# Passage into the second half: small weights ahead of the features, the features in four pieces, a layer's parameters four pieces ahead of their use

## The chip, the cores and the metric

The kernel runs on one core of one Trainium2 chip. A core has a matrix engine (PE, with its weight loads shown as PEld), three engines for elementwise work (DVE, ACT, POOL) and a sync engine, SP, whose queue issues nearly all transfers of this kernel. Each engine executes its own instructions in the order in which the program emitted them; they wait for each other through semaphores. Transfers are carried by 16 DMA engines that all queues share.

The metric is the time of one execution in device microseconds. Before the change it is 5200.37 us, the median of 3 runs (5200.36, 5200.37 and 5221.51).

## The reference

The input x has shape (4, 96, 64, 64). Four layers follow each other:

- Layer 0: two state-space (Mamba) blocks over the 4096 positions, then a 1x1 fusion. The fusion has a global part: the mean of x over the positions goes through `gp_w`, a ReLU and the second half of `fus_w`, and is added per image and channel. A batch norm over all images follows, with a residual:

```python
gp = relu(x.mean((2, 3)) @ gp_w.T + gp_b)
out = einsum('oc,bchw->bohw', fus_w, concatenate([mamba_out, broadcast(gp)], axis=1)) + fus_b
out = (out - mu) * rsqrt(var + EPS) * bn_g + bn_b + residual
```

- Layer 1: a group norm, a 3x3 mean pool (p), and a masked quadratic form over channels, added to its input. For each position and output channel o it sums `weight[o,c,d] * mask[o,c,d] * p[c] * p[d]`.
- Layers 2 and 3: tokens of 96 channels. An attention stand-in (layer norm, a linear map to 192 with batch norm and ReLU, an FFT over the tokens, a diagonal complex map with ReLU, the inverse FFT, a linear map back with batch norm), then a feed-forward part whose operands, weights and biases are rounded to 8-bit floats. Each layer i has its own parameters: `w1`, `w2`, the two batch norms `bn1` and `bn2` (gamma, beta, mean, variance), and the feed-forward weights `fw1`, `fw2` and biases `fb1`, `fb2`.

## The kernel before, in words

`tile_hybrid_kernel` has two halves. `_mamba` computes layer 0 up to the fused features and writes them to a DRAM tensor `fd[b]`, one per image b. `_back` does the rest. Their on-chip buffers come from pools that are closed and opened between the halves, and the first instructions of `_back` that touch a buffer start only when `_mamba` has ended.

**The passage.** `_back` begins with `begin()` (L695) and the first part of `norms(0, ...)` (L772). `begin()` emits, on SP, in this order: image 0's x in two halves (`xb`, L699), the features of image 0 as one transfer (`f`, L701), three 96x96 weights `gp_w`, `fus_g` and `grp` (L702 to L704, through the helper `_load` at L43, so the trace shows them at L45), then 32 loads of the quadratic form's weights and masks (L717), in eight groups of four. Then it emits the chain that makes the batch norm's scale `scl` and shift `shf`, mostly tiny DVE operations (L722 to L754) with two PE matmuls `p_g` (needs `gp_w`, L727) and `p_c` (needs `fus_g`, L731). Last, it emits on POOL, for each of the eight groups, two products of a weight and a mask and a sum (L758 to L760, called `wk`), with two clearings of the padded image `gpad` (L766) after the second group.

`norms(0)` then emits, for eight chunks of 512 columns, f = f * scl + x (DVE, L794) and the statistics of the result (L796), the group norm's scale and shift (L802 to L819, with `grp` in two matmuls), and for each of eight strips y a clearing of border rows on POOL (L838 for the first strip, L840 for the last), a copy into the padded image (ACT, L842), four DVE additions (L845 to L854) and two stores of the pooled strip to DRAM (L856). As soon as the first strip is pooled, `fill` (L863) can load shifted copies of it, the `cp` tiles (L873, L874), into 16 buffers.

**The products of image 0.** Layer 1 is computed as 37 products for each chunk of 512 positions. `product(n)` (L891) makes z for product n+3 on DVE (L887; L884 on ACT for one in 37), loads further `cp` tiles whose buffers are free, and emits the PE matmul of product n (L902), which the trace shows as two PE instructions. The z tiles have five buffers. An image has 8 chunks, so 296 products.

**The order around the change** is written out by hand, not planned: `together` (L1358) takes lanes of pieces and merges them by their relative position. For image 0 there are two lanes: the 296 products, and a side lane with the rest of `norms(0)` (36 pieces), `params(0)` (18), `params(1)` (18), `norms(1)` (61) and an empty stretch of weight 8. That makes 141 weights, so a piece of the side lane comes after every 296/141 = 2.10 products. `through(gen, n)` (L1370) cuts a generator at its `yield`s into n pieces, and the last piece runs whatever is left.

**A layer's parameters.** `params(i)` (L915) prepares one layer. Its pieces, counted by its `yield`s:

- piece 1: loads of `bn1` (L923), `w1` and `w2` (L924 and L925, shown at L45); piece 2 is empty;
- piece 3: 1/sqrt(var + eps) of bn1 times gamma, `s1` (`_rsqrt`, L611, then L929);
- piece 4: w1 times s1 (L932), a PE matmul that centres it (`p_c`, L934), its copy back on ACT (L935);
- piece 5: w1's bias row (L937, L938), load of `bn2` (L940); piece 6 is empty;
- piece 7: the same for bn2 (`s2`); piece 8: w2 times s2 and small vectors (L947 to L957);
- from piece 9: for fw1, fw2, fb1 and fb2 in turn, a load (L964), an empty piece, and two pieces later the rounding (two DVE casts, L968 and L970). The 18 pieces end during this: the last one loads fb2 and rounds it at once.

The loads go into temporary tiles with the tag `zz` (`hold`, L919), of which there are four buffers. `bn1` is loaded with one row per partition, 97 rows of 3072 bytes; `w1` with 97 rows of 768 bytes.

After image 0, the products of image b run beside the token layers of image b-1 (`layers`, L1333), and image 3's token layers run alone at the end.

Of the kernel before, what the change touches and what calls it, by code (L numbers as in the profile page):

```python
# [9 lines left out]
F32 = mybir.dt.float32  # L10
# [17 lines left out]
TC = 512  # L28
NCH = L // TC
H = 192  # L30
# [627 lines left out]
def _back(ctx, tc, io, w, fd, fstats, xsums, p2, out):  # L658
# [28 lines left out]
    def slot(name):  # L687
        return slots.tile([128, NJ * C], F32, name=name, tag="slot")
# [5 lines left out]

    def begin():  # L695

        xb = [slot(f"xb{h}")[0:C, 0 : L // 2] for h in range(2)]
        for h in range(2):
            nc.sync.dma_start(xb[h], io["x"][0][:, h * (L // 2) : (h + 1) * (L // 2)])  # L699
        f = feats[0] = feat.tile([C, L], F32, name="f_0", tag="f")  # L700
        nc.sync.dma_start(f, fd[0])  # L701
        c["gp_w"] = _load(nc, wp, io["gp_wT"], [C, C], "gp_w")  # L702
        c["fus_g"] = _load(nc, wp, io["fus_wT"][C : 2 * C, :], [C, C], "fus_g")
        c["grp"] = _load(nc, wp, io["k_group"], [C, C], "grp")  # L704


        free = [("cp", 0)] * NCP + [("zz", h) for _ in range(4) for h in range(2)] + [("n2", 0)] * 3 + [("z", 0)] * 5
        lds, zz = [], None
        for k0 in range(0, NE, KG):
            kn = min(KG, NE - k0)  # L710
            ld = []
            for m in ("bw1", "bm1", "bw2", "bm2"):
                tag, h = free.pop(0)
                if tag != "zz" or h == 0:
                    zz = tl(f"{m}_{k0}", [128, 2 if tag == "zz" else 1, TC], tag=tag)
                t = zz[:, h, 0 : kn * C].rearrange("p (k c) -> p k c", k=kn)
                nc.sync.dma_start(t, io[m][:, k0 : k0 + kn, :])  # L717
                ld.append(t)
            lds.append(ld)

        xsum = small("xsum")
        nc.vector.tensor_reduce(xsum, xsums, AX.X, ALU.add)  # L722
        fmv = wp.tile([C, B, 2], F32, name="fmv", tag="fmv")
        for b in range(B):
            nc.vector.bn_aggr(fmv[:, b, :], fstats[:, b])
        p_g = bank("s", [C, B], "p_g")
        nc.tensor.matmul(p_g, c["gp_w"], xsum, start=True, stop=True)  # L727
        gp = small("gp")
        nc.scalar.activation(gp, p_g, AF.Relu, bias=vec[:, _V_GPB : _V_GPB + 1], scale=1.0 / L)
# [12 lines left out]
        nc.vector.tensor_tensor(dv, dv, dv, ALU.mult)  # L742
        nc.vector.tensor_tensor(dv, dv, fmv[:, :, 1], ALU.add)
        var = small("var", 1)
        nc.vector.tensor_reduce(var, dv, AX.X, ALU.add)
        nc.vector.tensor_scalar(var, var, 1.0 / B, None, ALU.mult)
        rstd = _rsqrt(nc, work, var, [C, 1], "bn")
        c["scl"] = small("scl", 1)
        nc.vector.tensor_tensor(c["scl"], rstd, vec[:, _V_BNG : _V_BNG + 1], ALU.mult)
        c["shf"] = small("shf")  # L750
        nc.vector.tensor_scalar(c["shf"], cb, mu, c["scl"], ALU.subtract, ALU.mult)
        nc.vector.tensor_scalar(c["shf"], c["shf"], vec[:, _V_BNB : _V_BNB + 1], None, ALU.add)
        c["bias"] = small("bias")
        nc.vector.tensor_scalar(c["bias"], c["shf"], vec[:, _V_L1B : _V_L1B + 1], None, ALU.add)  # L754

        for n, ld in enumerate(lds):
            t = wp.tile([128, KG, C], F32, name=f"wk{n}", tag=f"wk{n}")[:, 0 : ld[0].shape[1]]
            nc.gpsimd.tensor_tensor(t, ld[0], ld[1], ALU.mult)  # L758
            nc.gpsimd.tensor_tensor(ld[2], ld[2], ld[3], ALU.mult)
            nc.gpsimd.tensor_tensor(t, t, ld[2], ALU.add)  # L760
            wk.append(t)
            if n == 1:
                c["gpad"] = []
                for i in range(2):
                    g = wp.tile([C, NY + 2, PW], F32, name=f"gpad{i}", tag=f"gpad{i}")
                    nc.gpsimd.memset(g, 0.0)  # L766
                    c["gpad"].append(g)
        return xb
# [146 lines left out]
    def params(i):  # L915

        d = {}

        def hold(name):  # L919
            return tl(f"{name}_{i}", [128, 2 * TC], tag="zz")  # L920

        bn1 = hold("bn1")[0 : C + 1, 0 : 4 * H].rearrange("p (a h) -> p a h", a=4)
        nc.sync.dma_start(bn1, io["bn1"][i])  # L923
        d["w1"] = _load(nc, wp, io["w1T"][i], [C + 1, H], f"w1_{i}")  # L924
        d["w2"] = _load(nc, wp, io["w2T"][i].rearrange("(h p) c -> p h c", h=2), [C, 2, C], f"w2_{i}")  # L925
        yield
        yield
        s1 = _rsqrt(nc, _Cut(hold("s1")), bn1[:, 3, :], [C + 1, H], f"s1_{i}")
        nc.vector.tensor_tensor(s1, s1, bn1[:, 0, :], ALU.mult)  # L929
        yield  # L930

        nc.vector.tensor_tensor(d["w1"][:C], d["w1"][:C], s1[:C], ALU.mult)  # L932
        p_c = bank("s", [C, H], f"p_c{i}")
        nc.tensor.matmul(p_c, tabs["ctr"], d["w1"][:C], start=True, stop=True)  # L934
        nc.scalar.copy(d["w1"][:C], p_c)  # L935
        yield
        nc.vector.tensor_tensor(s1, s1, bn1[:, 2, :], ALU.mult)  # L937
        nc.vector.tensor_tensor(d["w1"][C:], bn1[C:, 1, :], s1[C:], ALU.subtract)  # L938
        bn2 = hold("bn2")[0:C, 0 : 4 * C].rearrange("p (a h) -> p a h", a=4)
        nc.sync.dma_start(bn2, io["bn2"][i])  # L940
        yield
        yield
        s2 = _rsqrt(nc, _Cut(hold("s2")), bn2[:, 3, :], [C, C], f"s2_{i}")
        nc.vector.tensor_tensor(s2, s2, bn2[:, 0, :], ALU.mult)
        yield
        for h in range(2):
            nc.vector.tensor_tensor(d["w2"][:, h], d["w2"][:, h], s2, ALU.mult)  # L947
        d["sh2"] = wp.tile([1, C], F32, name=f"sh2_{i}", tag=f"sh2_{i}")
        nc.vector.tensor_tensor(d["sh2"], bn2[0:1, 2, :], s2[0:1], ALU.mult)
        nc.vector.tensor_tensor(d["sh2"], bn2[0:1, 1, :], d["sh2"], ALU.subtract)  # L950
        at = _V_ATT + i * 8
        for k, n in enumerate(("rd", "id", "rb", "ib")):
            d[n] = [vec[:, at + 2 * k + h : at + 2 * k + h + 1] for h in range(2)]
        for n, k, f in (("nid", 2, -1.0), ("rb2", 4, 2.0)):
            t = wp.tile([C, 2], F32, name=f"{n}_{i}", tag=f"{n}_{i}")
            nc.vector.tensor_scalar(t, vec[:, at + k : at + k + 2], f, None, ALU.mult)
            d[n] = [t[:, h : h + 1] for h in range(2)]  # L957
        yield

        def quantised(name, src, shape, dtype):  # L960
            n = math.prod(shape[1:])
            view = (lambda t: t) if len(shape) == 2 else (lambda t: t.rearrange("p (k c) -> p k c", k=shape[1]))
            t = view(hold(name + "f")[0 : shape[0], 0:n])
            nc.sync.dma_start(t, src)  # L964
            yield
            yield
            q = view(tl(f"hq_{name}_{i}", [128, NHC * TC], F8)[0 : shape[0], 0:n])
            nc.vector.tensor_copy(q, t, saturate=False)  # L968
            r = wp.tile(shape, dtype, name=f"{name}_{i}", tag=f"{name}_{i}")
            nc.vector.tensor_copy(r, q)  # L970
            d[name] = r
            yield

        yield from quantised("fw1", io["fw1T"][i], [C, HID], BF16)
        yield from quantised("fw2", io["fw2T"][i].rearrange("(h p) c -> p h c", h=NHC), [128, NHC, C], BF16)
        yield from quantised("fb1", io["fb1"][i], [128, NHC], F32)
        yield from quantised("fb2", io["fb2"][i], [128, 4 * C], F16)
        prm.append(d)

    def tables():  # L980
# [401 lines left out]
    with tc.manual_schedule():  # L1382
# [4 lines left out]
        for b in range(B):  # L1387
            lanes = [[(1.0, lambda n=n: product(n)) for n in range(b * NCH * NE, (b + 1) * NCH * NE)]]
            side = []
            if b == 0:  # L1390
                tables()
                side += through(opening, 36) + through(params(0), 18) + through(params(1), 18)
            else:
                lanes.append(idle(5.0) + layers(b - 1, False))
            if b + 1 < B:
# [165 lines left out]
```

## Time and profile before

The profiled execution took 5205.16 us; its span, from the first to the last instruction, is 5203.4 us. All positions below are in us from the start of that span.

| what | value |
|---|---|
| median of the runs | 5200.37 us |
| profiled execution, its span | 5205.16 us, 5203.4 us |
| busy share of the span: PE, DVE, ACT, POOL | 78%, 83%, 52%, 55% |
| passage, from the last store of `_mamba` to image 0's first product | 3052.3 to 3117.3 |
| products of image 0 | 3117 to 3418 |
| in that stretch: PE busy, DVE busy | 271.17 of 301 us, 257.65 of 301 us |
| the same, ACT and POOL busy | 22.22 us, 0.45 us |

A row of the timeline gives the start, the duration, the engine, the line, the operation, its output and inputs, and in brackets the idle time of the engine just before it with what ended the wait. SPq is the issuing of a transfer on SP, not the transfer. The chain of waits is followed back from the last instruction: at each step to what released it.

### The profile page before, as it was taken

Reading aid. Unit: us, or ns where it says so; the run is one execution under the profiler, and the core shown is the slowest. Engines: PE = TensorE matmul, PEld = TensorE weight load, DVE = VectorE, ACT = ScalarE, POOL = GpSimd, SP = SyncE. Lnnn points to the kernel's source line nnn. Section 1 sums busy time; section 2 is a strip of 40 time slices with the busy share of each in tenths; the row PEclk is TensorE's granted clock in tenths of the full one; section 3 lists DMA queues with packets and bytes.
Section 4 is the critical chain, followed back from the end, with each engine's and each line's share of the span. In section 5 each row is a group of like instructions: output and inputs, shape, how many; then the busy total and the mean of one; then the engine's idle time right before and its main releaser. Section 6 shows DMA issues by size and latency. Waiting matters only on the chain. (4 is left out here: it accounts for less than half of the span.)

```text
span 5203.4 us, 52872 instructions
## 1 busy us (share of the span) xinstructions
PE 4082.1 (78%) x15440; PEld 1752.6 (34%) x15440; DVE 4317.2 (83%) x5639; ACT 2680.5 (52%) x5149; POOL 2849.5 (55%) x2105
## 2 busy tenths in 40 slices
PE   4667877777777778777776728998898898989776
PEld 2222222222222222222222103345455454545565
DVE  2879999999999999999999778979787978787655
ACT  3555665656566665656565410025453444434566
POOL 2768888888888888888888650003130312212122
PEclk7777777777787777777786659999999999999877
DMA  4768888888988888898888754653324333232110
GB/s 111 170 157 207 194 202 206 195 206 194 214 193 201 200 204 206 194 213 191 203 198 207 171 144 142 194 152 94 105 79 145 94 92 111 87 94 81 47 33 21
DMA packets 314048, 800.20 MB, mean 154 GB/s; under 512 B 52247, under 2 KB 58106, under 8 KB 312702
## 3 DMA queue, kind: packets, MB, share of 16 engines
q1 hardware_dynamic: 310174, 790.53, 60.6%
q10 hardware_dynamic: 3584, 6.29, 0.4%
q8 instruction: 123, 2.02, 0.2%
q14 instruction: 167, 1.37, 0.1%
HBM read 703.83 MB, written 67.63 MB: 148 GB/s over the span
## 5 line engine op out<-in xcount | busy, mean ns | idle before, releaser
L475 POOL TENSOR_TENSOR hs<-hs,bc 128x1024 f32<-128x1024 f32 x767 | 1666.4, 2180 | 391.6 <-DVE hs L469 387.1
L469 DVE TENSOR_TENSOR_SCAN hs<-a,hst,pq 128x512 f32<-128x512 f32 x1280 | 1571.4, 1261 | 9.8 <-ACT a L452 9.8
L902 PE MATMUL py<-z,wk 128*96 128x512 f32 x2304 | 1114.8, 613 | 22.1 <-issue 14.3
L457 DVE TENSOR_TENSOR pq<-pq,bc 128x1024 f32<-128x1024 f32 x640 | 775.2, 1211 | 233.3 <-PE pq L447 233.2
L887 DVE TENSOR_TENSOR z<-cp,cp 128x512 f32<-128x512 f32 x1152 | 790.2, 711 | 185.9 <-PE py L902 173.4
L452 ACT ACTIVATE a<-a,aneg 128x512 f32<-128x512 f32 x1280 | 843.9, 711 | 38.4 <-DMA a<-ddl 33.1
L488 PE MATMUL py<-hs,red 128*32 128x512 f32 x3072 | 663.0, 855 | 29.8 <-POOL hs L475 29.5
L902 PEld LDWEIGHTS py<-z,wk 128*96 128x96 f32 x2304 | 366.9, 169 | 446.4 <-issue 315.1
L447 PE MATMUL pq<-uy,sel 64*128 64x512 f32 x768 | 258.2, 637 | 201.4 <-DVE hs L469 200.4
L1152 POOL MEMSET zz<- 96x2 f32 x16 | 1.6, 98 | 745.6 <-ACT zz L1161 651.8
L264 PE MATMUL mm_i<-hn,wk 97*128 97x512 f32 x512 | 322.8, 763 | 106.1 <-ACT xcv L275 80.9
L1253 POOL TENSOR_TENSOR o<-o,fb 128x384 f16<-128x384 f16 x64 | 70.0, 1094 | 546.6 <-ACT o L1258 493.3
L452 ACT ACTIVATE pq<-a,aneg 128x512 f32<-128x512 f32 x256 | 177.0, 692 | 334.0 <-DVE hs L469 322.8
L469 DVE TENSOR_TENSOR_SCAN hs<-pq,hst,db 128x512 f32<-128x512 f32 x256 | 323.7, 1264 | 3.5 <-POOL dx L303 1.5
L275 ACT ACTIVATE xcv<-mm_i,pvec 128x512 f32<-128x512 f32 x96 | 66.0, 687 | 493.4 <-DVE y L496 244.0
L457 POOL TENSOR_TENSOR db<-db,bc 128x1024 f32<-128x1024 f32 x128 | 301.6, 2356 | 14.3 <-DMA db<-ddu 14.3
L447 PE MATMUL pq<-ux,sel 64*128 64x512 f32 x512 | 175.6, 631 | 124.8 <-DMA ux<-ul 65.0
L447 PEld LDWEIGHTS pq<-uy,sel 64*128 64x128 f32 x768 | 98.9, 236 | 477.5 <-DVE hs L469 350.8
L264 PEld LDWEIGHTS mm_i<-hn,wk 97*128 97x128 f32 x512 | 106.8, 232 | 293.0 <-issue 161.0
L1184 PE MATMUL px<-bd,a 128*96 128x128 f32 x1024 | 147.6, 292 | 70.9 <-DVE a L1117 61.6
L1153 POOL TENSOR_TENSOR zz<-zz 96x256 f32<-96x256 f32 x128 | 122.6, 958 | 135.8 <-ACT zz L1160 83.6
L447 PEld LDWEIGHTS pq<-ux,sel 64*128 64x128 f32 x512 | 68.0, 229 | 326.4 <-DVE hs L469 178.8
(286 smaller groups left out, 6532.7 us busy)
## 6 DMA issues: line engine op xcount, KB each, us to landing
a<-ddl SPq DMA_DIRECT2D x768, 512.0 KB, 6.3
cp<-p SPq DMA_DIRECT2D x480, 192.0 KB, 2.7
db<-ddu SPq DMA_DIRECT2D x128, 512.0 KB, 8.3
bc<-ddb SPq DMA_DIRECT2D x64, 512.0 KB, 9.7
cp<-p SPq DMA_DIRECT2D x480, 64.0 KB, 2.7
ddl<-dl SPq DMA_DIRECT2D x128, 192.0 KB, 3.0
tw_k_fwd<-in_k_fwd SPq DMA_DIRECT2D x64, 256.0 KB, 3.3
tw_k_inv<-in_k_inv SPq DMA_DIRECT2D x64, 256.0 KB, 3.0
```

The source lines that it names most:

```text
L264: nc.tensor.matmul(p, wt[:, 0:128], hn_buf[bs[k], l][:, cols], **f)
L447: nc.tensor.matmul(pqs[s][:, i, :], sel[rows, r, :], made[unit][6][k][h][rows], start=True, stop=True)
L452: nc.scalar.activation(to[:, i, :], das[s][:, i, :], AF.Exp, scale=acol(s, i))
L457: engine.tensor_tensor(t, t, bc(unit, 2, k, h), ALU.mult)
L469: nc.vector.tensor_tensor_scan(hss[g][:, at, 1:], d0[:, i, :], d1[:, i, :], hst[pr, l, g % 12][:, at : at + 1], ALU.mult, ALU.add)
L475: (nc.gpsimd if s + 1 < n_steps else nc.vector).tensor_tensor(hs[:, :, :TC], hs[:, :, 1:], bc(unit, 3, k, h), ALU.mult)
L488: nc.tensor.matmul(pys[unit, k][32 * (i // 2 + i % 2 * 2) :][:32], red[:, r, :], hc[:, i, :TC], start=(r == 0), stop=(r == 3))
L887: nc.vector.tensor_tensor(zs[n], cps[q, r0], cps[q, r1], ALU.mult)
L902: nc.tensor.matmul(pys[q], wk[k // KG][:, k % KG, :], zs.pop(n), start=(k == 0), stop=(k == NE - 1))
L1153: nc.gpsimd.tensor_tensor(z0[:, :, 0, :], z0[:, :, 0, :], z1[:, :, 0, :], ALU.add)
L1184: nc.tensor.matmul(p[:, j, :], a2[i % 2][:, kk, :], tabs["bd"][:, int(kk > 0), :], start=True, stop=True)
L1253: nc.gpsimd.tensor_tensor(o2.rearrange("p j c -> p (j c)"), os.pop(g), d["fb2"], ALU.add)
```

## The change

It has two parts, both in `_back`.

In `begin()`, the three small weights are loaded first, ahead of x and f. The features f are loaded as four transfers of 1024 columns in place of one of 4096.

In `params(i)`, `bn2` is loaded with `bn1`, `w1` and `w2` in piece 1, behind them in SP's queue. Three empty pieces follow, so that `s1` is made in piece 5 in place of piece 3. w1 times s1 is piece 6, and the centring matmul piece 7, which also loads fw1. `s2` is piece 8. Piece 9 finishes w2 and loads fw2 and fb1; piece 10 rounds fw1 and loads fb2; fw2 is rounded in piece 11, fb1 in piece 12, fb2 in piece 14. Each `params` now gets 16 pieces of the side lane in place of 18, so the lane has 137 weights, one piece after every 296/137 = 2.16 products. The temporaries come from the same four `zz` buffers in a new order: bn1, bn2, s1, fw1, s2, fw2, fb1, fb2.

```diff
     def begin():
+        c["gp_w"] = _load(nc, wp, io["gp_wT"], [C, C], "gp_w")
+        c["fus_g"] = _load(nc, wp, io["fus_wT"][C : 2 * C, :], [C, C], "fus_g")
+        c["grp"] = _load(nc, wp, io["k_group"], [C, C], "grp")
         xb = [slot(f"xb{h}")[0:C, 0 : L // 2] for h in range(2)]
         for h in range(2):
             nc.sync.dma_start(xb[h], io["x"][0][:, h * (L // 2) : (h + 1) * (L // 2)])
         f = feats[0] = feat.tile([C, L], F32, name="f_0", tag="f")
-        nc.sync.dma_start(f, fd[0])
-        c["gp_w"] = _load(nc, wp, io["gp_wT"], [C, C], "gp_w")
-        c["fus_g"] = _load(nc, wp, io["fus_wT"][C : 2 * C, :], [C, C], "fus_g")
-        c["grp"] = _load(nc, wp, io["k_group"], [C, C], "grp")
+        for at in range(0, L, 2 * TC):
+            nc.sync.dma_start(f[:, at : at + 2 * TC], fd[0][:, at : at + 2 * TC])
...
-        bn1 = hold("bn1")[0 : C + 1, 0 : 4 * H].rearrange("p (a h) -> p a h", a=4)
-        nc.sync.dma_start(bn1, io["bn1"][i])
+        def load(name, src, shape):
+            view = (lambda t: t) if len(shape) == 2 else (lambda t: t.rearrange("p (k c) -> p k c", k=shape[1]))
+            n = math.prod(shape[1:])
+            t = view(hold(name)[0 : shape[0], 0:n])
+            nc.sync.dma_start(t, src)
+            return name, t, shape, n, view
+
+        def quantised(loaded, dtype):
+            name, t, shape, n, view = loaded
+            q = view(tl(f"hq_{name}_{i}", [128, NHC * TC], F8)[0 : shape[0], 0:n])
+            nc.vector.tensor_copy(q, t, saturate=False)
+            r = wp.tile(shape, dtype, name=f"{name}_{i}", tag=f"{name}_{i}")
+            nc.vector.tensor_copy(r, q)
+            d[name] = r
+
+        _, bn1, *_ = load("bn1", io["bn1"][i], [C + 1, 4, H])
         d["w1"] = _load(nc, wp, io["w1T"][i], [C + 1, H], f"w1_{i}")
         d["w2"] = _load(nc, wp, io["w2T"][i].rearrange("(h p) c -> p h c", h=2), [C, 2, C], f"w2_{i}")
-        yield
-        yield
+        _, bn2, *_ = load("bn2", io["bn2"][i], [C, 4, C])
+        for _ in range(4):
+            yield
         s1 = _rsqrt(nc, _Cut(hold("s1")), bn1[:, 3, :], [C + 1, H], f"s1_{i}")
         nc.vector.tensor_tensor(s1, s1, bn1[:, 0, :], ALU.mult)
         yield
         nc.vector.tensor_tensor(d["w1"][:C], d["w1"][:C], s1[:C], ALU.mult)
+        yield
         p_c = bank("s", [C, H], f"p_c{i}")
...
         nc.scalar.copy(d["w1"][:C], p_c)
-        yield
...
-        bn2 = hold("bn2")[0:C, 0 : 4 * C].rearrange("p (a h) -> p a h", a=4)
-        nc.sync.dma_start(bn2, io["bn2"][i])
-        yield
+        fw1 = load("fw1", io["fw1T"][i], [C, HID])
         yield
         s2 = _rsqrt(nc, _Cut(hold("s2")), bn2[:, 3, :], [C, C], f"s2_{i}")
...
         nc.vector.tensor_tensor(d["sh2"], bn2[0:1, 1, :], d["sh2"], ALU.subtract)
+        fw2 = load("fw2", io["fw2T"][i].rearrange("(h p) c -> p h c", h=NHC), [128, NHC, C])
...
-        yield from quantised("fw1", io["fw1T"][i], [C, HID], BF16)
-        yield from quantised("fw2", io["fw2T"][i].rearrange("(h p) c -> p h c", h=NHC), [128, NHC, C], BF16)
-        yield from quantised("fb1", io["fb1"][i], [128, NHC], F32)
-        yield from quantised("fb2", io["fb2"][i], [128, 4 * C], F16)
+        fb1 = load("fb1", io["fb1"][i], [128, NHC])
+        yield
+        quantised(fw1, BF16)
+        fb2 = load("fb2", io["fb2"][i], [128, 4 * C])
+        yield
+        quantised(fw2, BF16)
+        yield
+        quantised(fb1, F32)
+        yield
+        yield
+        quantised(fb2, F16)
+        yield
         prm.append(d)
...
-                side += through(opening, 36) + through(params(0), 18) + through(params(1), 18)
+                side += through(opening, 36) + through(params(0), 16) + through(params(1), 16)
```

More of the change, by code (lines that the diff above doesn't have):

```diff
@@ L957, in params @@
             d[n] = [t[:, h : h + 1] for h in range(2)]
+        fb1 = load("fb1", io["fb1"][i], [128, NHC])
         yield
[L960 to L972, printed above, removed]
-        yield from quantised("fw1", io["fw1T"][i], [C, HID], BF16)
-        yield from quantised("fw2", io["fw2T"][i].rearrange("(h p) c -> p h c", h=NHC), [128, NHC, C], BF16)
-        yield from quantised("fb1", io["fb1"][i], [128, NHC], F32)
-        yield from quantised("fb2", io["fb2"][i], [128, 4 * C], F16)
+        quantised(fw1, BF16)
[8 more added lines that the diff above has]
+        yield
         prm.append(d)
```

## The prediction

> **What bounds the kernel now.** I read the chain of waits first. It leads from the end back to what set it, so it tells whether the two places of the change lie on the path. Columns: start, length, what.
>
> ```profile
> 3055.49 15.74 DMA f<-fd
> 3074.95 4.96 DMA bw<-in_bw
> 3079.93 4.86 DMA bw<-in_bw
> 3084.80 1.77 DVE f L794
> ...
> 3105.32 0.88 ACT gpad L842
> ...
> 3185.67 13.82 DMA bn<-in_bn
> ...
> 3231.62 14.08 DMA bn<-in_bn
> ...
> 3279.10 3.98 DMA fb2f<-in_fb
> ```
>
> Both do: the features' load, both bn1 loads, and fb2's. So time saved there counts, until another wait takes over. The stretches of the products of image 0 and of image 1 (busy time of PE, PEld, DVE, ACT, POOL, then PE's clock, DMA share, GB/s):
>
> ```profile
> 3117.00:3418.00 301.00, 271.17 (x622) 100.85 (x623) 257.65 (x459) 22.22 (x34) 0.45 (x3) 0.95 0.56 169
> 3418.00:3950.00 532.00, 473.38 (x2093) 271.30 (x2093) 432.09 (x879) 232.23 (x530) 106.61 (x102) 0.96 0.38 113
> ```
>
> PE sets the pace: 90% and 89% busy, at nearly full clock. A product is two PE instructions of 0.43 us: 222 of them take 95.36 us in the chain, so 0.86 us a product. Where PE stands still inside image 0, by its timeline:
>
> ```profile
> 3204.95 0.95 PE L934 MATMUL p_c<-w,tctr 96*96 96x192 f32 x2 [13.09 <-DVE w L932]
> 3235.75 1.96 PE L902 MATMUL py<-z,wk 128*96 128x512 f32 x4 [0.82 <-DVE z L887]
> 3251.21 0.96 PE L934 MATMUL p_c<-w,tctr 96*96 96x192 f32 x2 [10.06 <-DVE w L932]
> 3284.51 1.10 PE L902 MATMUL py<-z,wk 128*96 128x512 f32 x2 [2.42 <-DVE z L887]
> ```
>
> 13.09 + 0.82 + 10.06 + 2.42 = 26.4 us, all from the parameters: DVE waits for a load, and the z tiles queue behind it. The cause of the two long ones, in the timeline, and then a 2 us window (columns as in the stretches above):
>
> ```profile
> 3185.67 0.27 SPq L923 DMA_DIRECT2D bn<-in_bn  x1
> 3185.99 2.89 SPq L45 DMA_DIRECT2D w<-in_w1T  x1
> 3188.92 8.46 SPq L45 DMA_DIRECT2D w<-in_w2T  x1
> 3199.52 0.26 DVE L614 TENSOR_SCALAR s<-bn 97x192 f32<-97x192 f32 x1 [9.99 <-DMA bn<-in_bn]
> ```
>
> ```profile
> 3192.00:3194.00 2.00, 0.00 (x0) 0.00 (x0) 0.00 (x0) 0.00 (x0) 0.00 (x0) 1.00 0.06 26
> ```
>
> bn1 is used 13.85 us after its issue. Meanwhile the DMA share is 0.06, one engine of 16, at 26 GB/s: 298 KB / 26 GB/s = 11.5 us[...].
>
> For the passage, the POOL and ACT timelines:
>
> ```profile
> 3072.87 1.19 POOL L758 TENSOR_TENSOR wk<-bw,bm 128x480 f32<-128x480 f32 x1 [28.75 <-DMA bm<-in_bm]
> 3104.15 0.15 POOL L838 MEMSET gpad<- 96x66 f32 x1
> 3105.32 0.87 ACT L842 ACTIVATE gpad<-f,gs,gn_r 96x576 f32<-96x576 f32 x1 [1.82 <-DVE gs L819]
> 3106.27 0.82 DVE L845 TENSOR_TENSOR rows<-gpad 96x640 f32<-96x640 f32 x1 [1.04 <-ACT gpad L842]
> ```
>
> POOL works without a gap from 3072.87 and reaches the border clearing L838 at 3104.15. DVE's chain ends with gs at 3105.23, ACT copies at 3105.32. The two chains arrive within 1 us of each other; the chain of waits shows only the later one.
>
> [...] The change keeps the 97 rows, so bn1 stays that slow. [...] POOL's wk operations go from 1.19 to about 1.64 us while L794 runs, and tiny DVE steps take 1.0 to 1.2 us in place of 0.15. [...] Here the clock drops to 0.50 some 4 us into the first stall; ten matmuls after the second take 6.47 us, not 4.3.
>
> **Part 1, the passage.** All of it starts at 3054.44, when SP may first issue (the last store of the first half has landed; DVE's first operation of the second half starts then too). Three issues, 0.47 + 0.49 + 0.57 = 1.5 us, move in front of x; xb, f and the wk loads slip by that. gp_w's wait behind 3 MB goes: p_g ran at 3071.64, and a small load takes about 2.5 us (fb1: issued 3227.95, used 3230.49), so p_g comes at about 3057 and cb at 3058.5. The 19 DVE steps to L754 took 3073.01 to 3084.87 beside POOL; without POOL they are 0.19 us apart (3076.58, 3076.77, 3076.95), 3.6 us, with ACT's root about 4: ready at 3063. Then L794 waits for f. xb's halves freed later loads at 3061.1 and 3064.6, f at 3071.25: with 1.5 us of slip and quarters of 1.67 us, f's parts land at about 3067.7, 3069.4, 3071.1, 3072.7. The split itself I price by image 1's features, also four transfers, issued from 3423.18 and moved at about 250 GB/s against f's 235: 0 to -0.4 us. Eight chunks of L794 and L796 at 1.4 to 1.6 us from 3067.7 end at 3079; gs came 6.6 us after the last one, so at about 3086, 19 us earlier than before.
>
> But L838 comes after the wk operations in POOL's order, and the strip's first addition L845 reads the border it clears. POOL starts when the first bw and bm land: slip 1.5 us, less some 0.8 us, because the small weights no longer travel between f and them, +0.6. It took 31.3 us; of eight L794 steps that cost it 3.5 us (eight operations in 12.9 us, not 9.4), some five now run before it starts, -2.0. L838 ends at 3104.3 + 0.6 - 2.0 = 3102.9. If the copy L842 waits for it, 3105.32 - 3103.0 = 2.3 us are gained; if only L845 does, 3106.27 - 3103.0 = 3.2. The trace doesn't tell which; I take **-2.7**, and as ends +1 (POOL slips 1.5 and gains nothing) and -5.5 (f and the wk loads flow faster by 2 to 3 us). The other 16 us turn into idle DVE time behind POOL.
>
> **Part 2, bn1.** The load to use distance goes from 2 pieces at 2.10 products to 4 at 2.16: 4.2 to 8.6 products, 4.4 more, at 0.69 to 0.86 us: 3.0 to 3.8 us. Before, DVE reached L614 3.86 us after the issue for layer 2; for layer 3, 7.7 us, of which 2.2 were the wait for fb2, which goes. So both arrive at about 7.5, and wait 13.85 - 7.5 = 6.3 us (before: 9.99 and 6.37). PE's stall is that, plus the root's chain (3.9 us, L614 to L929), plus one z (0.7), less PE's stock. The stock was 2.3 us (DVE stops at 3189.53, PE at 3191.86), and a finished z lay behind p_c, 0.6 to 0.9 us; with p_c a piece later PE uses it, 2.9 in all. 6.3 + 3.9 + 0.7 - 2.9 = 8.0 us each, 16 for 13.09 + 10.06 = 23.15: **-7.2**. The clock still drops in 8 us, so the slow matmuls after it stay. Ends: -4 (DVE arrives at 6) to -11 (at 9.5).
>
> **Part 3, fb2.** Loaded and rounded in one piece, it stopped PE 0.82 and 2.42 us. Now four pieces lie between, 7.4 us, against 3.2 to 4.0: **-3.2**, and -2.4 if the first is taken up by bn1.
>
> **At no cost.** fw1, fw2 and fb1 have 3, 2 and 3 pieces; fw2's 3.7 us cover its 3.3 (3270.41 to 3273.67) barely, which costs 1 us of DVE if missed, inside PE's stock. bn2 goes behind w2's issue on SP: SP is held 12.2 us in place of 11.6, and the cp loads behind it. Chunk 2's cp loads are all emitted before piece 1 (a buffer of the chunk before is free by product 73, piece 1 comes at 79), and after the hold SP waited until 3205.5 for DVE anyway. fw2's load waits for DVE's last read of bn2 (same buffer), fb2's for fw1's rounding; both are short steps that DVE is doing at that moment. No operation is added on DVE, PE or ACT.
>
> Sum: -2.7 - 7.2 - 3.2 = -13.1 us. The profiled execution took 5205.16 us (span 5203.4), so it would be 5192; the median was 4.8 us lower, 5200.4 - 13.1 = **5187**. PE stays busy to 3418 and after, so I let the lead through whole.
>
> **Rivals.**
> A, the border doesn't hold the strip (POOL free earlier, or no dependence in time): the passage gains the whole 19 us less half a us, total 18.5 + 10.4 = 29 us, 5171. Against it: one POOL queue, L838 last in it. 0.05.
> B, the waits take the gain back: bn1 comes no earlier, so if DVE arrives at 6 us and POOL slips 1.5 us, it is -4 - 2.4 + 1 = -5, 5195. For it: the landing is fixed by one DMA engine. 0.25.
> C, slower, by SP: four loads in a burst hold its queue 12 us, then fw2 and fb2 wait there for DVE; cp tiles come late and z waits for them. It costs one us for each us past a cp tile's first use, and decides from 13 us in all, some 6 for each layer: then 5205; I have seen no z wait for cp after 3126 beyond 3 us. 0.05.
> D, the change doesn't do what it says: gp_w, although first, waits with everything for 3054.44; that is already in the sum. Only if it landed behind x would part 1 lose its lead, and POOL hides that: 5189. It goes with the forecast.
>
> **How the numbers follow.** Forecast (5182 to 5192) 0.65, B 0.25, A 0.05, C 0.05. Forecast and B hold 0.9; with the ends of the parts (-5.5 - 11 - 3.2 = -20 if all are good, half of it likely to miss) the range is 5176 to 5198. Half a per cent, 26 us, is about what a measurement of this kernel can tell from no change: below 5174.4 is faster, A alone and not all of it, 0.05; above 5226.4 is slower, a C twice as bad, 0.03; the rest 0.92.
>
> **What would show it.** p_g near 3057; L794 started by f's first part near 3068; gs near 3086, and L842 or L845 waiting for POOL L838 near 3103. PE's stalls before the z after s1 about 8 us twice, none at fb2; bn1 still 13.8 us at 0.06 of the DMA. It is wrong if the strip starts before 3100, if PE's stalls add up to under 10 or over 20 us, or if z waits for cp.

## The result and the profile after

The changed kernel takes **5181.68 us** (median of 7 runs, 5171.03 to 5194.18), against 5200.36 us for the kernel before (7 runs, 5187.16 to 5221.51): a ratio of 0.9966, with a 95% interval of 0.9945 to 0.9988. That is 18.7 us less, where 13.1 was forecast; in the interval, 6 to 29 us. The profiled execution of the changed kernel took 5181.68 us, its span 5179.9.

Two spans can't simply be subtracted here. The first half, which the change doesn't touch, ended at 3052.29 us in the profile before and at 3043.50 in the one after, and anywhere from 3029.53 to 3063.08 in the runs below. Everything is therefore measured from the last store of the first half (the issue of the last store to `fd`), and the time after it is cut at two points: the first product of image 0, and PE's first transposition of normalised tokens (`plt`, L1108 in the kernel before), a little behind the last product of image 0. Inside the products, "idle" is the time in which PE has no matmul (3.5 us of it, in every run, stand right before `plt`), and "slow clock" is PE's busy time times one minus the granted clock, summed over windows of 1 us. The kernel before was profiled twice, the changed kernel once (all in us):

| kernel | passage | products | of it idle | of it slow clock | the rest | last store to end |
|---|---|---|---|---|---|---|
| before | 65.0 | 311.9 | 33.0 | 6.8 | 1774.2 | 2151.1 |
| before, second profile | 64.8 | 318.3 | 34.8 | 11.9 | 1771.3 | 2154.5 |
| after | 61.3 | 303.7 | 23.4 | 9.2 | 1771.4 | 2136.4 |

After minus the mean of the two: passage -3.6, products -11.4, rest -1.4, in all -16.4 us. What neither idles nor runs at a slow clock is 271 to 273 us in every run of this study, so the products are a constant plus PE's waits and its slow clock.

The chain of waits of the changed kernel (start, length, what):

```profile
3092.89 0.59 POOL wk L761
3093.48 0.10 POOL gpad L839
3093.58 11.24 issue
...
3174.29 14.68 DMA bn<-in_bn
...
3217.59 14.86 DMA w<-in_w2T
...
3257.82 4.31 DMA fr<-fd
```

In place of the features' load it now runs through POOL's products and its border clearing. Layer 2's load of bn1 is still on it. For layer 3 the chain names w2, issued in the same group, which landed at 3232.45, 3.9 us after bn1; DVE's timeline shows its wait there for bn1 (below) and none for w2. In place of fb2 there is another load, image 1's features `fr`.

The passage, from the PE, DVE, ACT and POOL timelines of the changed kernel:

```profile
3047.50 0.45 PE L728 MATMUL p_g<-xsum,gp_w 96*96 96x4 f32 x2 [6.73 <-DMA gp_w<-in_gp_wT]
3057.97 0.75 DVE L795 SCALAR_TENSOR_TENSOR f<-f,scl,xb 96x512 f32<-96x512 f32 x1 [4.85 <-DMA f<-fd]
3079.82 0.87 ACT L843 ACTIVATE gpad<-f,gs,gn_r 96x576 f32<-96x576 f32 x1 [4.90 <-DMA bw<-in_bw]
3093.42 0.15 POOL L839 MEMSET gpad<- 96x66 f32 x1
3093.60 0.82 DVE L846 TENSOR_TENSOR rows<-gpad 96x640 f32<-96x640 f32 x1 [13.87 <-POOL gpad L839]
```

The chain of scale and shift starts 4.0 us after the last store in place of 19.4, and DVE's first chunk 14.5 us after the last store in place of 32.5. The copy into the padded image (ACT) starts 36.3 us after the last store in place of 53.0. Then the strip's first addition stands for 13.87 us, until POOL has cleared the border: 16.7 us of lead, of which 3.9 reach the addition.

PE inside image 0's products, by its timeline:

```profile
3193.55 2.02 PE L903 MATMUL py<-z,wk 128*96 128x512 f32 x2 [7.47 <-DVE z L888]
3233.19 2.02 PE L903 MATMUL py<-z,wk 128*96 128x512 f32 x2 [7.43 <-DVE z L888]
3263.63 2.02 PE L903 MATMUL py<-z,wk 128*96 128x512 f32 x2 [2.85 <-DVE z L888]
```

The two stalls of bn1 shrink from 13.09 and 10.06 us to 7.47 and 7.43; fb2's two are gone, and a third stall of 2.85 us has come. The cause of the third is in the DVE timelines. Below are the waits of the changed kernel, and then the last wait of fb2 in the kernel before:

```profile
3189.00 0.26 DVE L614 TENSOR_SCALAR s<-bn 97x192 f32<-97x192 f32 x1 [6.47 <-DMA bn<-in_bn]
3228.57 0.26 DVE L614 TENSOR_SCALAR s<-bn 97x192 f32<-97x192 f32 x1 [6.38 <-DMA bn<-in_bn]
3262.23 0.75 DVE L795 SCALAR_TENSOR_TENSOR fr<-fr,scl,xr 96x512 f32<-96x512 f32 x1 [5.01 <-DMA fr<-fd]
```

```profile
3283.10 0.36 DVE L968 CAST hq_fb<-fb2f 128x384 fp8e5<-128x384 f32 x1 [3.06 <-DMA fb2f<-in_fb]
```

`fr` is fetched at the end of the parameters and used one piece later. Before, fb2's wait of 3.06 us and its rounding lay between the fetch and its use, and `fr` landed under them. Without them DVE stands at `fr` from 3257.22, just before SP issues its load (3257.82), and waits out the whole landing, 4.4 us from the issue.

What SP does for a layer's parameters, by its queue in the changed kernel:

```profile
3174.29 0.24 SPq L927 DMA_DIRECT2D bn<-in_bn  x1
3174.57 3.17 SPq L45 DMA_DIRECT2D w<-in_w1T  x1
3177.79 7.59 SPq L45 DMA_DIRECT2D w<-in_w2T  x1
3185.48 2.01 SPq L927 DMA_DIRECT2D bn<-in_bn  x1
```

bn1 is used 14.7 us after its issue. A 2 us window while it travels reads, in the columns of the stretches above:

```profile
3184.00:3186.00 2.00, 2.00 (x5) 0.49 (x3) 0.00 (x0) 0.00 (x0) 0.00 (x0) 1.00 0.06 26
```

A share of 0.06 again, that of one engine of 16, at 26 GB/s.

### The profile page after: what moved, and what is told of

Same layout as the page of the kernel before. It is cut to its first block, busy times and chain, and to the rows that moved or that the text cites. A ratio compares the mean times of both kernels' runs of the same rounds, so it can differ in the third digit from the quotient of the medians.

```text
span 5179.9 us, 52879 instructions
## 1 busy us (share of the span) xinstructions
PE 4071.0 (79%) x15440; PEld 1748.3 (34%) x15440; DVE 4310.7 (83%) x5639; ACT 2682.0 (52%) x5149; POOL 2848.9 (55%) x2105
## 5 line engine op out<-in xcount | busy, mean ns | idle before, releaser
L469 DVE TENSOR_TENSOR_SCAN hs<-a,hst,pq 128x512 f32<-128x512 f32 x1280 | 1571.2, 1261 | 10.3 <-ACT a L452 10.3
L903 PE MATMUL py<-z,wk 128*96 128x512 f32 x2304 | 1119.7, 615 | 53.0 <-issue 30.3
L264 PEld LDWEIGHTS mm_i<-hn,wk 97*128 97x128 f32 x512 | 104.3, 226 | 289.9 <-issue 155.8
```

What stands on the lines that cost most here:

```text
L264: nc.tensor.matmul(p, wt[:, 0:128], hn_buf[bs[k], l][:, cols], **f)
L469: nc.vector.tensor_tensor_scan(hss[g][:, at, 1:], d0[:, i, :], d1[:, i, :], hst[pr, l, g % 12][:, at : at + 1], ALU.mult, ALU.add)
L903: nc.tensor.matmul(pys[q], wk[k // KG][:, k % KG, :], zs.pop(n), start=(k == 0), stop=(k == NE - 1))
```

## The experiments

Times of different experiments can't be compared directly: in the runs beside them the kernel before took anything from 5176.75 to 5226.16 us. So a ratio is to the kernel before as it ran beside the experiment, and a time of one run decides nothing; there the profile's stretches carry the reading.

The theory: the gain is DVE reaching bn1 later and POOL being finished earlier, and bn1's landing on one DMA engine (the share of 0.06) and the border clearing are what holds back more. The rivals: that the passage does the work, that the waits only move, that DVE's lead is worth nothing even with POOL out of its way.

### The two parts apart

The passage part alone is the kernel before with the new `begin()`; the parameters part alone is the changed kernel with the old one. The diff of either is one half of the diff of the change.

> The passage part alone; the parameters stay as before. I measure two stretches that don't depend on how long the first half took: the passage (issue of the last store of the fused features to PE's first product; before 65.0 us, both parts 61.3) and the products of image 0 (first product to the first token transposition; before 311.9, both parts 303.7). Theory (POOL's queue holds the strip): passage 61.3, products 312, so about 4 us faster than before. Rival 1 (the passage carries most of the gain of 18.7 us, the stretches mislead): 12 us or more faster. Rival 2 (nothing, POOL slips with the loads): passage 64 to 66.

> The parameters' part alone; the passage stays as before. Theory: passage 65.0, products 303.7, PE waits of about 7.5 us at both layers' z after s1 and one of about 2.9 us for image 1's first chunk; about 8 us faster than before, and with the passage part alone the two add up to the whole. Rival (most of the gain sits in the passage): products within 3 us of 311.9.

Measured beside each other: the passage part alone 5199.07 us (14 runs; ratio to before 1.0002, 0.9987 to 1.0017), the parameters part alone 5186.44 us (22 runs; 0.9973, 0.9961 to 0.9985). In the profiles the passage part shortens the passage to 61.6 us, and the parameters part leaves it at 64.3 and cuts PE's idle time in the products from 33.0 to 22.9. With the parameters part, last store to end is 2132.2 us, even less than with both parts (2136.4), so a difference of a few us between two single profiles doesn't show an effect. The products of the passage part alone, however, took 317.4 us, 5.5 more than before: 2.4 of it idle, 3.3 slow clock. Either the passage part costs the products what it saves, or the one profile of before was a good one. A second profile of both decides.

> The same kernel as the one with the passage part alone, once more. If its missing gain was chance in the clock: passage again 61.5 us (65.0 before), PE idle in products 33 to 35 us, the part lost to the slow clock anywhere from 4 to 10 us, so that last store to end is 2145 to 2150 us. If the passage part itself slows the products: products again 317 us and the slow-clock part again about 10 us.

> The kernel before, unchanged, profiled a second time, to see how much of its products' 311.9 us is its own. Against it stand two profiles of the passage part alone with 317.4 and 316.6 us: there fw2 landed 4.8 and 4.9 us after its issue in place of 3.3, and the last stall of the parameters, 2.6 and 2.7 us in place of 2.4, was followed by 4 us at half clock. If the passage part causes this: fw2 again lands within 3.3 us, DVE waits 1.7 us for it, products 311 to 313 us. If it is chance of the landing and the clock: fw2 may land anywhere from 3.3 to 5 us, products anywhere from 311 to 317 us, and what follows image 0's products takes 1765 to 1774 us as in the other runs.

The passage part alone, second profile: passage 61.5 us, products 316.6, idle 35.0, slow clock 9.4, which is what the "slows the products" side had said. The kernel before, second profile: products 318.3, idle 34.8, slow clock 11.9. So the passage part isn't needed for these losses: the kernel before shows them without it. Two things vary between runs. fw2 of layer 3 lands 3.3 us after its issue in the first profile of before, and 5.2 in the second (4.8 and 5.0 with the passage part); and the same stall may or may not be followed by a slow clock. Two windows right behind fb2's last stall, which is 2.42 us in both profiles of before, first then second:

```profile
3284.50:3287.00 2.50, 2.49 (x6) 1.06 (x7) 2.50 (x5) 0.00 (x0) 0.00 (x0) 1.00 0.05 16
```

```profile
3286.46:3289.00 2.54, 2.54 (x4) 0.98 (x5) 2.54 (x5) 0.00 (x0) 0.00 (x0) 0.63 0.00 0
```

The column after POOL's is PE's clock: 1.00 in one run, 0.63 in the other, and four matmuls in the time of six. In this stretch the slow clock costs 4.0 to 11.9 us in the profiles of this study, up to nearly 4% of the products and more than either of the small terms of the forecast.

With both profiles of each, last store to end is 2151.1 and 2154.5 us for before, 2149.9 and 2146.9 for the passage part: its 3.4 us are there in the passage, and too small for the measured ratio, whose interval reaches 6.8 us below no change.

### What holds the passage

Without the clearing of the first strip's border for image 0. The padded image has been cleared as a whole before, so nothing is left out of the computation.

```diff
-            if y == 0:
+            if y == 0 and xb is None:
                 nc.gpsimd.memset(g[:, 0, :], 0.0)
```

> The changed kernel without the border clearing of image 0's first strip (the padded image has just been cleared whole, so nothing is left out of the result). Theory (that clearing, last in POOL's queue, is what the first strip waits for): the first addition of the strip follows ACT's copy at once, some 12 us earlier, passage 61.3 - 12 = about 49 to 51[...], about 11 us faster than the changed kernel. Rival (the copy's or the weights' own readiness holds it): passage stays within 2 us of 61.3.

Measured: 5183.34 us (22 runs; 0.9962, 0.9950 to 0.9974), passage 59.4 us. The theory said 49 to 51 and was wrong. The addition of the run without the clearing shows why:

```profile
3094.44 1.80 DVE L846 TENSOR_TENSOR rows<-gpad 96x640 f32<-96x640 f32 x1 [9.61 <-POOL wk L759]
```

It starts 45.9 us after the last store in place of 50.1, but still waits 9.61 us for POOL, now for a product of the weights. The additions' output `rows` has the tag `n2`, and the `n2` buffers serve before that as landing places of the weights' and masks' loads, in the seventh of the eight groups (the list `free`). So `rows` may be written only when POOL has read them. The clearing hid a second dependence on POOL, 4.2 us ahead of it; 1.9 of them reach the passage, because the additions now run beside POOL (1.80 us for the first in place of 0.82). In the next kernel, which has no second clearing either, the loads take the `n2` and `z` buffers first, so that POOL reads them first:

```diff
-        free = [("cp", 0)] * NCP + [("zz", h) ...] + [("n2", 0)] * 3 + [("z", 0)] * 5
+        free = [("n2", 0)] * 3 + [("z", 0)] * 5 + [("cp", 0)] * NCP + [("zz", h) ...]
```

> The changed kernel without the border clearing of image 0's first strip, and with the weight loads' borrowed buffers in another order: first the three of tag n2 and the five of z, then the cp and zz ones. Without the clearing alone the strip still waited for POOL's seventh group, whose loads sit in the n2 buffers that the strip's sums reuse. Theory: with n2 free after the first group, the strip's first addition follows ACT's copy, about 37 us after the last store, slower beside POOL (6 us in place of 3), the strip is stored at 43, PE's first product comes at 51 to 53 us in place of 61.3. Rival (a third dependence, such as the cp buffers that POOL's groups 3 to 6 now hold, takes over): passage over 57.

Measured: 5166.74 us in one run, passage 51.0 us. The addition now follows the copy:

```profile
3081.48 0.87 ACT L843 ACTIVATE gpad<-f,gs,gn_r 96x576 f32<-96x576 f32 x1 [4.90 <-DVE gs L820]
3082.38 0.96 DVE L846 TENSOR_TENSOR rows<-gpad 96x640 f32<-96x640 f32 x1 [0.98 <-ACT gpad L843]
```

The lead that the small weights and the split features give was held by two dependences on POOL, not by one, and is worth another 10.3 us (61.3 to 51.0) once both are gone; the products stay at 302.0.

How much of it is the split: the changed kernel with the features as one transfer, `nc.sync.dma_start(f, fd[0])` in place of the loop of four.

> The changed kernel with the features as one transfer. Theory (POOL holds the strip, the split only shifts DVE's work out of POOL's way): L794's first chunk starts about 5 us later than in the changed kernel (20 in place of 14.5 us after the last store), more of its eight steps run beside POOL, POOL's weight chain takes 30.5 to 31.5 us in place of 29.2, the passage is 1 to 2 us longer (62.5 to 63.5). Rival (the split carries the passage's gain): passage 65 or more.

Measured: 5185.63 us in one run, passage 61.9 us, where 62.5 to 63.5 were expected. DVE's first chunk starts 19.4 us after the last store in place of 14.5, and POOL takes 30.3 us in place of 29.2 for its products: seven of DVE's eight chunks fall beside them in place of three, and six of POOL's operations take 1.52 to 1.65 us in place of three, where the full-sized others take 1.19 or 1.20. With POOL in the way the four pieces are worth 0.6 us at most: another run with the pieces (image 1's features used later, below) also has a passage of 61.9. The copy into the padded image starts 44.3 us after the last store in place of 36.3, so the pieces may be worth more once POOL is out of the way; no run shows that.

### What holds the parameters

A lead of eight pieces for bn1 in place of four, with 20 pieces of the side lane for each `params`:

```diff
-        for _ in range(4):
+        for _ in range(8):
             yield
...
```

> The changed kernel with eight empty pieces between bn1's load and its root in place of four (and 20 pieces a layer in place of 16). Theory (PE's wait = landing 14 us - lead + root's chain 3.9 + one z 0.7 - PE's stock): the lead grows by 4 pieces, some 8.4 products at 0.86 us = 7 us, DVE's wait at the root (6.4 us) goes to 0, PE's two waits go from 7.5 to about 1 to 2 us, and below that it can't go, since the root's chain itself holds DVE for longer than PE's stock lasts. Rival (DVE can't run ahead, or SP's hold starves the z of cp tiles): PE's waits stay over 4 us, or move to a z that waits for cp.

Measured: 5165.49 us in one run, products 288.9 us, idle 12.1. One wait of bn1 is left:

```profile
3191.42 0.26 DVE L614 TENSOR_SCALAR s<-bn 97x192 f32<-97x192 f32 x1 [2.55 <-DMA bn<-in_bn]
```

PE stands for 3.56 us there, and for 0.96 and 1.60 us in layer 3, where 1 to 2 us were expected for both layers. The wait for `fr` fell to 0.69 us as well.

bn1 and w1 without the 97th row in their transfers. With 97 rows bn1 travelled at a DMA share of 0.06, before and after the change; that 96 rows would travel at more was the author's estimate. bn1 is loaded as 96 rows and one. w1 is loaded with 96 rows; its last row is computed later anyhow, so it isn't read.

```diff
-        _, bn1, *_ = load("bn1", io["bn1"][i], [C + 1, 4, H])
-        d["w1"] = _load(nc, wp, io["w1T"][i], [C + 1, H], f"w1_{i}")
+        bn1 = hold("bn1")[0 : C + 1, 0 : 4 * H].rearrange("p (a h) -> p a h", a=4)
+        nc.sync.dma_start(bn1[0:C], io["bn1"][i][0:C])
+        nc.sync.dma_start(bn1[C:], io["bn1"][i][C:])
+        d["w1"] = wp.tile([C + 1, H], F32, name=f"w1_{i}", tag=f"w1_{i}")
+        nc.sync.dma_start(d["w1"][0:C], io["w1T"][i][0:C])
```

> The changed kernel, with bn1 loaded as 96 rows and one row apart, and w1 as 96 rows (its 97th row is written by DVE later, so it needs no load). Theory (97 rows go to one DMA engine, and that sets bn1's landing): bn1 lands 3 to 5 us after its issue, DVE does not wait at the root of bn1 any more, SP issues w1 and w2 in under 1 us each in place of 3 and 7.5, PE's two waits of 7.5 us fall to about 1.7 each (root's chain 3.9 + one z 0.7 - PE's stock 2.9), products 303.7 - 11.6 = 292. Some 11 us faster than the changed kernel. Rival (the 14 us are latency or a full queue behind the strips' stores): bn1 still takes 12 us or more, no gain.

Measured: 5171.93 us (12 runs; 0.9951, 0.9930 to 0.9971), products 289.0 us where 292 were expected, idle 12.8. SP's queue of this run:

```profile
3160.38 0.40 SPq L939 DMA_DIRECT2D bn<-in_bn  x1
3160.82 0.31 SPq L940 DMA_DIRECT2D bn<-in_bn  x1
3161.17 0.32 SPq L942 DMA_DIRECT2D w<-in_w1T  x1
3161.53 0.42 SPq L45 DMA_DIRECT2D w<-in_w2T  x1
```

And the windows behind the issue, in the columns of the stretches:

```profile
3161.01:3162.01 1.00, 1.00 (x3) 0.33 (x2) 1.00 (x3) 0.00 (x0) 0.00 (x0) 1.00 0.98 275
3165.01:3166.01 1.00, 1.00 (x4) 0.35 (x3) 0.83 (x2) 0.00 (x0) 0.00 (x0) 1.00 0.00 0
```

The DMA share, 0.98 just behind the issue (a store of the strip, issued 0.5 us ahead of bn1, falls there too), is 0.00 at 4.6 us after it: by then bn1, w1, w2 and bn2 have landed, within the expected 3 to 5 us. One engine at the 26 GB/s of the changed kernel would still have been busy with bn1 (298 KB / 26 GB/s = 11.5 us), so more than one carried the 96 rows; how many isn't shown. DVE uses bn1 8.1 us after the issue (3160.38 to 3168.51) and doesn't wait. The long issues are gone too: w1 and w2 together hold SP for 0.7 us in place of 10.8. PE idles 10.6 us less than in the changed kernel, about as much as with the lead of eight pieces (11.3). The run moves bn1, w1 and w2 at once, so it doesn't tell whether w2, which landed 3.9 us behind bn1 in layer 3 of the changed kernel, would have held DVE next.

fb2 alone, in the kernel before: its load is issued behind fb1's, three pieces ahead of where it was.

```diff
+            if name == "fb1":
+                ahead["fb2"] = hold("fb2f")[0:128, 0 : 4 * C]
+                nc.sync.dma_start(ahead["fb2"], io["fb2"][i])
...
```

> The kernel before, with one thing changed: fb2 is loaded together with fb1, three pieces ahead of its rounding. Theory (fb2's wait of layer 3 covered the landing of image 1's first chunk, which is loaded right behind it): the waits of 0.82 and 2.42 us at fb2 go, and PE waits 2 to 3 us at the first chunk of image 1 (DVE at the chunk's first operation waits 3 to 5 us for the load), so that only 0.8 to 1.2 us of the 3.2 are gained. Rival (the wait at image 1's chunk comes from the new side lane of 137 weights): no such wait, 3.2 us gained.

Measured: 5209.01 us in one run, products 313.4 us, idle 34.2, against 33.0 and 34.8 in the two profiles of before: no gain is seen, where 0.8 to 1.2 us were expected. fb2's waits are gone, and others are longer:

```profile
3252.96 0.26 DVE L614 TENSOR_SCALAR s<-bn 97x192 f32<-97x192 f32 x1 [9.10 <-DMA bn<-in_bn]
3293.09 0.75 DVE L794 SCALAR_TENSOR_TENSOR fr<-fr,scl,xr 96x512 f32<-96x512 f32 x1 [1.75 <-DMA fr<-fd]
```

Layer 2's fb2 gave its wait of 2.2 us to layer 3's bn1 (6.37 and 6.79 us before), whose landing this kernel leaves as it was; layer 3's gave part of its own to `fr` (1.75 us, and 1.58 us of PE, where 3 to 5 and 2 to 3 were expected). The time that fb2 had cost was time in which another load came in.

The last wait, `fr`, in the changed kernel: four empty pieces between the fetch and the first use, taken from the empty stretch behind.

```diff
-        yield
+        for _ in range(1 if b != 1 else 5):
+            yield
...
```

> The changed kernel, with four empty pieces put between the fetch of image 1's features and their first use (and taken from the empty stretch behind). Theory (part 3's gain went into the wait for that fetch, because DVE no longer spends 3.06 us on fb2 just before it): the DVE wait for fr falls from 5.01 us to under 1, PE's wait of 2.85 us at image 1's first chunk goes, PE's idle time in image 0's products falls from 23.4 to 20 to 21 us, and the two bn1 waits of PE stay at 7 to 7.5 us. Rival (the wait would turn up at the next fetch or at the chunk's end): idle time stays at 23 us.

Measured: 5185.32 us in one run; PE's idle time 20.7 us in place of 23.4, inside the 20 to 21 that were expected. The first chunk of `fr` no longer waits; a later one waits 2.12 us, and PE stands for 1.00 and 0.42 us there. bn1's stalls are 6.61 and 6.85 us, a little under the expected 7 to 7.5. So of the 2.7 us less idle time only 1.9 are `fr`'s (2.85 + 0.45 before, 1.00 + 0.42 now); the rest is bn1's stalls, which without this change were already anything from 6.8 to 7.5 us in the other runs with four pieces of lead and 97 rows.

### All repairs together

> The changed kernel with all four repairs at once: 96+1 rows for bn1 and w1, no second clearing of the border, the buffer order of the run with n2 and z first, and the later use of image 1's features. Nothing is left out of the computation. If the gains add up: passage about 51 us (61.3 in the changed kernel), PE idle in image 0's products about 10 us (23.4), products 285 to 289 us with the clock's part, last store to end about 2107 us (2136 in the changed kernel, 2151 before), time about 5160 us, ratio to before 0.991 to 0.993. If DVE's lead in the passage is only lent (PE later waits for something else): products over 295 us and the ratio about that of the rows alone, 0.995.

Measured: **5161.37 us** (6 runs, 5148.71 to 5174.46), beside 5194.36 us for the kernel before (11 runs): ratio 0.9926, 0.9897 to 0.9955. That is less time than before, beyond the interval; against the changed kernel's 0.9945 to 0.9988 the two intervals still overlap a little, and the profile speaks for it: last store to end 2106.0 us in place of 2136.4. Passage 51.0 us, products 289.9, idle 12.5, slow clock 4.1. No wait for bn1 is left on DVE, and one of 1.84 us for `fr`. Idle time came out 2.5 us above the expectation: besides the 3.5 us before `plt`, PE still stands ten times, for 0.2 to 1.8 us, most of it behind z's that queue after the root chains (0.97 and 1.59 us in layer 2, 0.96 and 1.34 in layer 3), after a wait of DVE for image 1's x (1.46) and at its statistics (1.77). The passage is 10.3 us shorter and the products 13.8, as in the runs apart, so DVE's lead in the passage isn't lent. The other 6.3 of the 30.4 us lie in the rest, which no repair aims at and which was anything from 1765.1 to 1774.2 us in the 14 profiles.

## Why the prediction was right, and where it was not

The time (5182 in 5176 to 5198) and the sign came out as forecast, and the middle was 5.3 us too high, well inside the scatter of the measurement. Part of that is luck: part 3 gave 2.3 us less than its price, and parts 1 and 2 gave 2.0 more. By its steps:

**Part 1, the passage: -2.7 forecast, -3.6 measured.** The mechanism held: the border clearing L838 (L839 in the changed kernel) holds the strip, and the rest of DVE's lead is idle. Its open choice, whether the copy or only the addition waits, is settled: the copy doesn't, so it was the 3.2 us end. POOL's first product slipped by 0.16 us in place of 0.6 (20.74 us after the last store, 20.58 before), and POOL's work fell from 31.28 to 29.18 us, by 2.1 where 2.0 were forecast. Two figures off the path missed: L795 came 14.5 us after the last store (forecast 15.4), and gs 2.5 us later than forecast, so the lead was 16.7 us and not 19. The forecast took over gs's 6.6 us behind the last chunk, measured where POOL was done before their last steps; with POOL busy throughout they became 9.8.

**Rival A** stated the whole lead as the gain if the border didn't hold the strip. The runs show that its condition was incomplete: the buffers of `rows` hold the strip just as well. With both gone the passage gains 14 us in all, not 18.5: the copy comes 17.1 us earlier, and the four additions beside POOL take 5.9 us in place of 3.1.

**Part 2, bn1: -7.2 forecast, -8.25 measured, -9.1 against the second profile of before** (13.49 + 10.49). DVE arrived 8.2 and 8.4 us after the issue (forecast 7.5), and bn1 was used 14.7 us after it (forecast 13.85, layer 2's figure before; layer 3's had been 14.1). The two misses cancel, which is luck: DVE waited 6.47 and 6.38 us, forecast 6.3. For layer 3 the forecast's own terms, 7.7 - 2.2 + 3.0 to 3.8, give 8.5 to 9.3 and not 7.5. The rest of the difference is PE's stock: 6.47 + 3.9 + 0.7 - 7.47 = 3.6 us of work ahead, not 2.9.

**Part 3, fb2: -3.2 forecast, -0.9 measured (-1.8 against the second profile of before); this step failed.** The load is off DVE's way as forecast, and PE's 0.82 and 2.42 us with it. But the step priced only the wait that it removed, and didn't ask what had been landing under it: the `fr` fetch, issued just behind. Counting all of PE's waits from layer 2's fb2 to image 1's first chunks, before had 0.82 + 2.42 + 0.97 = 4.21 us (second profile 0.79 + 1.85 + 2.42 = 5.06), after has 2.85 + 0.45 = 3.30. The runs on fb2 alone and on `fr` alone show both sides of it: earlier fb2 gains nothing that the profiles can show where another load is next, and later use of `fr` gives 1.9 us back.

**What was costed at nothing** stayed so: no wait of DVE for fw1, fw2, fb1 or fb2 is recorded after the change, and none for cp once the first chunk runs. SP is held 13.2 us by the four loads (3174.29 to 3187.49), forecast 12.2; rival C's starving of z doesn't appear. Its 5205 us doesn't follow from its terms either: 13 us lost cancel the 13.1 gained and leave the time where it was.

**The clock.** In the profile before, the clock fell to 0.50 2.7 us into PE's first stall (3191.86 to 3194.57), not some 4 as the prediction read from windows of 2 us, and even a stall of 2.22 us (features whole) was followed by a drop. The step of the prediction that counts on it, slow matmuls after stalls of 8 us, isn't touched by that: behind the changed kernel's stall of 7.47 us the granted clock stayed at 0.50 for 4.8 us.

**The sum.** -3.6 for the passage and -10.5 of idle time in the products are 14.1 us, against 13.1 forecast. What the measurement shows beyond it, to 16.4 in the profiles and 18.7 in the medians, is no more than the variation of the clock's part (4 to 12 us) and of the first half; what it consists of stays open. The part that carries the time is the parameters (0.9973 alone); that the passage part counts for its 3.4 us rests on profiles, not on a ratio.

## What to carry to other kernels

Before an engine's wait for a load is priced as a gain, look at the next loads that the engine uses: what landed under the wait becomes the next wait, by its landing time minus the engine's new arrival (here 5.01 us for `fr`, once fb2's 3.06 us were gone). A dependence that ends last can hide a second one almost as late, here a buffer shared by tag and free 4.2 us earlier, so after taking one away in thought, walk through every input, output and buffer of the waiting instruction. And when a load travels at the share of one DMA engine, as bn1 did here with 97 rows (0.06, 26 GB/s), splitting off the odd row can gain as much as doubling the lead (10.6 and 11.3 us of PE's idle time here), and frees the issuing queue besides (w1 and w2 held it 0.7 us in place of 10.8).

## What the runs showed of the hardware

- In the changed kernel a transfer of w1 with 97 rows and the w2 transfer behind it hold SP's queue for 3.1 to 3.2 and 7.3 to 7.6 us of issuing, and bn2 behind them for 2.0 to 2.1 us. With bn1 and w1 loaded as 96 rows, w1 and w2 take 0.3 to 0.4 us each.
- The same stall of 2.42 us was followed by full clock (1.00) in one run of the kernel before and by 0.63 in another. A stall of 2.44 us (no second clearing) was followed by full clock, one of 2.22 us (features whole) by a drop to 0.50 that began 1.3 us after PE had resumed. Stalls of 2.6 and 2.7 us (the passage part alone, its two profiles) and of 2.85 us (the changed kernel) were each followed by 3 to 4 us at a granted clock of 0.50 or near it; one such drop costs 1.4 to 1.7 us.
- The first half ended at 3029.5 to 3063.1 us in 14 profiles of kernels that don't differ in it.
- A load of 144 KB (fw2), with the same transfers issued around it, took 3.3 us in one run of the kernel before and 5.2 in the next.
